# Graph attention and slice attention on one core: tokens interleaved by four, two more transposes by blocks and DMA, a new planner

## The chip, the cores and the metric

The kernel runs on one core of a Trainium2 chip. A core has TensorE (PE, matmuls, with a separate path PEld that loads weights), VectorE (DVE), ScalarE (ACT), GpSimd (POOL) and SyncE (SP, which here only issues DMAs). All run their own instruction queues in order and wait for each other by semaphores. The metric is device time in microseconds (us). The time before is 2927.27 us, the median of 3 runs (2927.26 to 2929.62).

## The reference

`x` has 32 batches of 512 tokens with 256 features, all in float32. Each batch goes through a graph block and a slice-attention block, each with a residual. Cut to what matters:

```python
# graph block, on xn = layernorm(x)
out = relu(xn @ mlp1_w + mlp1_b);  residual = out              # 256 -> 512
h = out @ W_fc                                                 # 512 -> 512
att = softmax(leaky_relu(f1[:, :, None] + f2[:, None, :]))     # f1, f2: h times halves of a_fc
out = elu(elu(att @ h)) + residual
out = relu(out @ mlp2_w + mlp2_b);  residual = out             # 512 -> 256
h = out @ W_hand
e = where(adj > 0, leaky_relu(f1[:, :, None] + f2[:, None, :]), -9e15)
x = x + relu(elu(elu(softmax(e) @ h)) + residual)
# slice block, on xn = layernorm(x), 8 heads, 64 slices each
w = softmax((xn @ W_x + b_x) @ W_slice / temperature)          # 512 tokens x (8 heads x 64 slices)
token = (w.T @ (xn @ W_fx + b_fx)) / (sum of w over tokens)
out_slice = softmax(q @ k.T / 8) @ v                           # q, k, v from token, per head
x = x + (w @ out_slice) @ W_out + b_out
```

Outputs are all of `x`, in float32.

## The kernel before

**Tiling.** A batch's 512 tokens are four tiles of 128 (`NT = 4`), tile `t` holding tokens `t*128` to `t*128+127`. Tensors exist with tokens on the partitions (`xn`, `h`, `e`, `w`, `u`) or with features on them (`xnT`, `o0T`, `o1T`, `o2T`, `xn2T`, `wT`, with 512 token columns). A matmul contracts over partitions, so several tensors must be transposed. Weights are folded at the start: `weff`, `beff` (W_x with W_slice), `wqk`, `wvo` (W_v with W_out), and the columns of `wfc` and `wh` that give f1 and f2.

**Stages of a batch**, in the order in which the code records them:
- `front(b)`: load (`xt`), layernorm to `xn`, transpose to `xnT`; mlp1 to `o0T` (lines 606 to 613); `h` (616 to 627); the factors `fm`, `f2m`, `ex`, `acb`, with transposes on TensorE (628 to 657); `pT`, the unnormalised attention of the first graph layer, from two products on VectorE (659 to 667); attention times h and the double elu to `u` (671 to 682), transposed and added to `o0T` to give `o1T` (683 to 687).
- `middle(b)`: mlp2 to `o2T`; `h` of the second layer (`h2`); `f2b`, a broadcast row made by four TensorE transposes; the residual `r2`, `o2T` transposed back by eight TensorE transposes (717 to 723); per tile of tokens `e` on VectorE, its exp on ScalarE, and four TensorE transposes and a copy into `p2T` (728 to 743); p2T times h, elu, and the sum into `x1`.
- `back(b)`: layernorm, `xn2T` by eight TensorE transposes, the slice weights `w` with their softmax, `wT` by 16 TensorE transposes; the sums `s1` over tokens, `s1T` by eight TensorE transposes; the token block `pm` (lines 832 to 839): for each of four head pairs `p` and two `k` a matmul of 128 x 128, of which only the two 64 x 64 diagonal blocks are used, and one bias matmul from the four rows of `bfx` and `nrow`; then scores `psc`, `attbd`, `vo`, `gg`, and the output.

**Transposes through DRAM.** `xn` and `u` are transposed without TensorE: `flip` (line 355) is one VectorE instruction that transposes each 32 x 32 block inside 128 x 256 or 128 x 512, writing runs of 32 elements; `gather` (361) then writes the four groups of 32 partitions with four DMAs into a scratch tensor in DRAM and reads them back with one, so that the blocks land in their places. The token columns come back in the order (a t i), and `in_order` and `as_gathered` are views that read them in the order needed.

**What sets the order.** No engine order is written out by hand. `Recorder` records every operation, and `_schedule` (115) simulates the engines with the costs of `_cost` (90), list scheduling by a key. The key is the batch number plus a share of the batch's TensorE work; `order` (227) tries 45 combinations of three parameters (`ORDERS`) and takes the one with the shortest `_length`. A DMA is reckoned as 0.1 us on its issuer and a landing after 2.5 us plus its bytes over 180 GB/s, each alone. `AHEAD = 3` lets a batch start while the oldest unfinished is up to three behind. The program is emitted in that order, with semaphores (line 255, so all instructions carry this line in the profile).

**Queues.** All loads of `x`, all scratch DMAs and the output are issued by SP, in the planned order: an issue that waits holds back all that follow. Some weights are loaded from ScalarE's queue at the start. PSUM has five `mm` buffers, two `tr` and one `sm`.

Of the kernel before, what the change touches and what calls it, by code (L numbers as in the profile page):

```python
# [14 lines left out]
ENGINES = ("tensor", "vector", "scalar", "gpsimd", "sync")  # L15
P = 128
# [4 lines left out]
class Recorder:  # L21
# [4 lines left out]
    DRAIN = 0.17  # L26
    KEPT = 1
    AHEAD = 3
    ORDERS = (1.0, 1.1, 1.2, 1.3, 1.4), (1.2, 1.4, 1.6), (0.0, 0.1, 0.2)

    def __init__(self, nc):
        self.nc, self.ops, self.logs, self.age, self.stage = nc, [], {}, -1, 0
        for engine in ENGINES:
            setattr(self, engine, _Recording(self, engine))
# [24 lines left out]
    def take(self, engine, method, args, kwargs):  # L59
# [4 lines left out]
        op = _Op(engine, method, args, kwargs, self.age, self.stage, len(self.ops))  # L64
        op.cost, op.lag = self._cost(op, outs[0], ins)
        before = {}
        for aps, writes in ((ins, False), (outs, True)):
            for ap in aps:
# [4 lines left out]
                op.logs.add(log)  # L73
# [16 lines left out]
    def _cost(self, op, out, ins):  # L90
# [6 lines left out]
        if op.method == "dma_start":  # L97
            return 0.1, 2.5 + out.size() * 4 / 180e3
        if op.engine == "tensor":
            one = max(n / 1200 + 0.002, 0.109)  # L100
            return (one if op.method == "transpose" else 2 * one), self.DRAIN
# [13 lines left out]
    def _schedule(self, ops, key, spare):  # L115
# [34 lines left out]
        done = []  # L150
        while len(done) < len(ops):
# [22 lines left out]
            free[op.engine] = t + op.cost  # L174
            for log in op.logs:
                users[log] -= 1
                until[log] = max(until[log], op.end)
                if not users[log]:
                    slots[log.tag].append(until[log] + self.SIGNAL + spare)
# [17 lines left out]
    def _length(self, ops):  # L197

        free, ready, users, until, slots, held = {}, {}, {}, {}, {}, set()
        for op in ops:  # L200
            for log in op.logs:
                users[log] = users.get(log, 0) + 1
        for op in ops:
            at = ready.get(op, 0.0)
            for log in op.logs:
                if log not in held:
                    held.add(log)
                    places = slots.setdefault(log.tag, [0.0] * log.bufs)
                    places.sort()
                    at = max(at, places.pop(0))  # L210
            t = free.get(op.engine, 0.0)
            t = max(t + (0.03 if op.engine == "tensor" and at > t - 0.1 else 0.0), at)
            free[op.engine], end = t + op.cost, t + op.cost + op.lag
            for log in op.logs:
                users[log] -= 1
                until[log] = max(until.get(log, 0.0), end)
                if not users[log]:
                    slots[log.tag].append(until[log] + self.SIGNAL)
            for later in op.after:
                if later.engine != op.engine:  # L220
                    at = end + self.SIGNAL
                else:
                    at = t + op.cost if op.engine == "tensor" else end
                ready[later] = max(ready.get(later, 0.0), at)
        return max(free.values())

    def order(self):

        work, parts = {}, {}
        for op in self.ops:
            stage = op.age, op.stage
            parts[op] = work.get(stage, 0.0)
            work[stage] = parts[op] + (op.cost if op.engine == "tensor" else 0.0)
        best = None
        for late, long, spare in product(*self.ORDERS):
            turns = {
                op: op.age + (late + long * part / work[op.age, 1] if op.stage else
                              part / (work[op.age, 0] or 1.0))  # L240
                for op, part in parts.items()
            }
            try:
                ops = self._schedule(self.ops, turns.get, spare)
            except RuntimeError:
                continue
            length = self._length(ops)
            if best is None or length < best[0]:
                best = length, ops
        self.length = best[0]  # L250
        return best[1]
# [6 lines left out]
class _Log:  # L258


    def __init__(self, ap, age):
        tensor = ap.tensor
        self.name, self.tag, self.bufs = tensor.name, tensor.tag, tensor.tag_meta.bufs
        self.psum = ap.space == bass.MemoryType.PSUM

        self.queue = self.tag, age if self.psum else 0
        self.entries = []


class _Op:  # L270
    def __init__(self, engine, method, args, kwargs, age, stage, index):
        self.engine, self.method, self.args, self.kwargs = engine, method, args, kwargs
        self.age, self.stage, self.index = age, stage, index
        self.logs, self.after = set(), []
# [17 lines left out]
def adj_ffn_kernel(  # L292
# [59 lines left out]

    Q = 32

    def flip(src, stage, t):

        nc.vector.transpose(
            stage[:, :, ts(t, Q)], src.rearrange("p (c i) -> p c i", i=Q)
        )

    def gather(stage, dst):


        blocks = stage.shape[1]
        scr = dram.tile([blocks, Q, P // Q, P], F32, name="scr", tag=f"scr{blocks}", bufs=2)
# [8 lines left out]
    def in_order(cols):  # L374

        return cols.rearrange("p (a t i) -> p t a i", a=P // Q, t=NT)

    def as_gathered(cols):

        return cols.rearrange("p (t a i) -> p a t i", a=P // Q, t=NT)  # L380
# [4 lines left out]
    def row(name, shape=(P, 512)):  # L385
        return new(name, shape, bufs=2)
# [11 lines left out]
    def load_x(b):  # L398
        if b < B:
            xt[b] = new("xt", [P, NT, D], bufs=2)  # L400
            nc.sync.dma_start(xt[b], x[b].rearrange("(t p) d -> p t d", p=P))
# [14 lines left out]
    for s in range(2):  # L416
        nc.scalar.dma_start(
            wfc[:, :, s, :HH], W_fc[:, ts(s, HH)].rearrange("(k p) f -> p k f", p=P)
        )
    w2 = new("w2", [P, KH, D])  # L420
# [5 lines left out]
    nc.sync.dma_start(wh[:, :, :D], W_hand.rearrange("(k p) f -> p k f", p=P))  # L426
    wfx = new("wfx", [P, KD, INNER])
# [27 lines left out]

    for a, width in ((a_fc, HID), (a_hand, D)):
        ab = med("ab", (P, 2, HID))
        nc.sync.dma_start(
            ab[:, :, :width],
            bass.AP(tensor=a.tensor, offset=a.offset, ap=[[0, P], [width, 2], [1, width]]),  # L460
        )
        for k in range(width // P):
            for s in range(2):
                scr = row("m")
                if width == HID:
                    w_k, wa = wfc[:, k, :, :HH], wfc[:, k, s, HH : HH + 1]
                    a_s = ab[:, s, :].rearrange("p (s f) -> p s f", s=2)
                    scr_k = scr.rearrange("p (s f) -> p s f", s=2)
                else:
                    w_k, wa = wh[:, k, :D], wh[:, k, D + s : D + s + 1]  # L470
                    a_s, scr_k = ab[:, s, :D], scr[:, :D]
                nc.vector.scalar_tensor_tensor(
                    scr_k, w_k, 1.0, a_s, op0=OP.mult, op1=OP.mult, accum_out=wa
                )

    adjt = new("adjt", [P, NT, N], tag="w", dtype=I32)
    nc.sync.dma_start(adjt, adj.rearrange("(t p) j -> p t j", p=P))
    for t in range(NT):
        nc.vector.tensor_scalar(mbias[:, t, :], adjt[:, t, :], 0.0, None, op0=OP.is_gt)
# [95 lines left out]
    def transpose_features(src, dst):  # L575

        for k in range(KD):
# [3 lines left out]
            nc.scalar.copy(dst[:, k, :], pt)  # L581
# [13 lines left out]
    def front(b):  # L595

        load_x(b + 1)
        xn = new("xn", [P, NT, D])
        layernorm(xt[b], xn, "ln1")
        stage = new("xn_stage", [P, D // Q, P])  # L600
        for t in range(NT):
            flip(xn[:, t, :], stage, t)
        xnT = new("xnT", [P, KD, N])
        gather(stage, xnT)
        o0T = new("o0T", [P, KH, N], bufs=2)
        for m in range(KH):
            pm = mm_tile([P, N])
            for k in range(KD):
                nc.tensor.matmul(
                    pm.rearrange("p (t a i) -> p t a i", t=NT, i=Q), w1[:, k, ts(m)],  # L610
                    in_order(xnT[:, k, :]), start=(k == 0), stop=(k == KD - 1),
                )
            nc.scalar.activation(o0T[:, m, :], pm, AF.Relu, bias=b1[:, m : m + 1])


        h = new("h", [P, NT, 2, HH + 1])
        for t in range(NT):
            for s in range(2):
                pm = mm_tile([P, HH + 1])
                for k in range(KH):  # L620
                    nc.tensor.matmul(
                        pm, o0T[:, k, ts(t)], wfc[:, k, s, :], start=(k == 0), stop=(k == KH - 1)
                    )
                if s:
                    nc.vector.tensor_copy(h[:, t, s, :], pm)
                else:
                    nc.scalar.copy(h[:, t, s, :], pm)
        f1, f2 = h[:, :, 0, HH], h[:, :, 1, HH]

# [28 lines left out]

        pT = new("pT", [P, NT, N])
        for j in range(NT):  # L660
            nc.vector.tensor_scalar(
                pT[:, j, :], acb[:, 1, :], ex[:, 3, j : j + 1], None, op0=OP.mult
# [5 lines left out]

        o1T = new("o1T", [P, KH, N])
        stage = new("u_stage", [P, HID // Q, P], tag="p2T")  # L670
        for i in range(NT):
# [11 lines left out]
            flip(u, stage, i)  # L683
        gather(stage, o1T)
        for m in range(KH):
            o1 = o1T[:, m, :].rearrange("p (a t i) -> p a t i", t=NT, i=Q)
            nc.vector.tensor_tensor(o1, o1, as_gathered(o0T[:, m, :]), op=OP.add)
        return o1T

    def middle(b, o1T):  # L690

        o2T = new("o2T", [P, KD, N])
        for m in range(KD):
            pm = mm_tile([P, N])
            for k in range(KH):
                nc.tensor.matmul(
                    pm.rearrange("p (t a i) -> p t a i", t=NT, i=Q), w2[:, k, ts(m)],
# [271 lines left out]
```

## Time and profile before

| what | us |
|---|---|
| median of three runs | 2927.27 |
| the profiled execution's own time | 2928.26 |
| its span, first to last instruction | 2926.5 |
| TensorE busy with matmuls | 2853.9 |
| VectorE busy | 1978.3 |
| ScalarE busy | 1119.3 |
| mean granted TensorE clock | 0.996 of full |

Rows of the page that matter for the change, each with count, busy us and mean ns of one:

| engine, row | count | busy us | mean ns |
|---|---|---|---|
| PE `tr<-ident,e` | 512 | 76.8 | 273 |
| PE `tr<-ident,o2T` | 256 | 43.6 | 273 |
| PE `mm<-s1T,wfx` | 512 | 80.9 | 275 |
| PE `mm<-nrow,bfx` | 64 | 35.9 | 640 |
| DVE `u_stage<-u` (flip, 128x512) | 128 | 88.9 | 695 |
| DVE `xn_stage<-xn` (flip, 128x256) | 128 | 49.0 | 421 |
| DVE `pT<-acb,ex` | 128 | 55.8 | 478 |
| DVE `h<-mm` 128x257 | 128 | 54.4 | 425 |
| DVE `h<-mm` 128x258 | 64 | 27.3 | 426 |
| ACT `p2T<-tr` | 128 | 74.9 | 585 |
| ACT `r<-tr` | 64 | 37.4 | 585 |

A matmul of float32 shows as two instructions on TensorE, a transpose as one. The mean of one includes the time in which it overlaps its neighbours in the pipeline, so the distance between starts is shorter than the mean. "Idle before" is time of that engine alone; only idle time of the engine that bounds the kernel costs time.

### The profile page before, as it was taken

How to read it: one execution, taken by the hardware profiler on the slowest of the kernel's cores; microseconds unless marked ns; L12 is line 12 of the kernel's file. 1: busy time of each engine (PE TensorE's matmuls, PEld its weight loads, DVE VectorE, ACT ScalarE, POOL GpSimd, SP SyncE). 2: the span in 40 equal slices, each digit the busy share in tenths (PEclk: the TensorE clock that was granted, in tenths of full speed). 3: DMA queues.
4: the chain of work that ended last, by engine and by line, in shares of the span. 5: the costliest groups of instructions: out<-in, count | busy, mean ns of one | idle time of the engine just before them, and what ended most of it. 6: DMA issues, size and time to landing. Idle time of an engine off the chain costs nothing.

```text
span 2926.5 us, 35159 instructions
## 1 busy us (share of the span) xinstructions
PE 2853.9 (98%) x13037; PEld 2187.4 (75%) x13037; DVE 1978.3 (68%) x4694; ACT 1119.3 (38%) x2182; POOL 112.8 (4%) x233
## 2 busy tenths in 40 slices
PE   3999999999999999999999999999999999999997
PEld 3777777777778777778777778777777777777775
DVE  4567776667776666776676866677766677766675
ACT  1433444333443343443333443333433334433432
POOL 1000000000000000000000000000000000000000
PEclk9999999999999999999999999999999999999998
DMA  5112220112211122211122211122201122201110
GB/s 177 44 29 65 65 65 22 52 57 65 65 53 34 44 65 65 65 44 44 44 65 65 65 36 51 44 65 65 65 26 54 51 65 65 61 19 45 43 44 15
DMA packets 185412, 159.34 MB, mean 54 GB/s; under 512 B 9109, under 2 KB 159257, under 8 KB 185241
## 3 DMA queue, kind: packets, MB, share of 16 engines
q1 hardware_dynamic: 181904, 154.96, 18.0%
q10 hardware_dynamic: 3336, 2.14, 0.3%
q8 instruction: 103, 1.69, 0.2%
q14 instruction: 69, 0.56, 0.1%
HBM read 89.96 MB, written 67.11 MB: 54 GB/s over the span
## 4 chain that ended last, share of the span: by engine, by line
PE 95%; DVE 3%; DMA 1%; ACT 0%; issue 0%; SPq 0%; POOL 0%; ACTq 0%; POOLq 0%; DVEq 0%
PE mm L255 85%; PE tr L255 9%; PE sm L255 1%; DVE w L255 1%; DVE mx L255 0%; DVE rs L255 0%; DMA wfx<-in_L_ffn_W_fx_dram 0%; DMA temp<-n_L_ffn_temperature_dram 0%; DVE m L255 0%; DVE u L255 0%; DMA scr<-xn_stage 0%; ACT m L255 0%; DMA xt<-in_x_dram 0%; DVE pT L255 0%; DVE ln_st L255 0%
## 5 line engine op out<-in xcount | busy, mean ns | idle before, releaser
L255 PE MATMUL mm<-wfc,o0T 128*128 128x257 f32 x2048 | 579.0, 381 | 0.0
L255 PE MATMUL mm<-h,pT 128*128 128x257 f32 (+1 forms) x2048 | 454.6, 378 | 0.1
L255 PEld LDWEIGHTS mm<-h,pT 128*128 128x128 f32 x2048 | 386.1, 189 | 80.5 <-issue 13.4
L255 PEld LDWEIGHTS mm<-wfc,o0T 128*128 128x128 f32 x2048 | 363.7, 190 | 53.2 <-issue 16.3
L255 PE MATMUL mm<-gg,wT 128*128 128x256 f32 x1024 | 299.5, 379 | 0.0
L255 PE MATMUL mm<-h,p2T 128*128 128x256 f32 x1024 | 290.8, 379 | 0.0
L255 PE MATMUL mm<-xnT,w 128*128 128x512 f32 x512 | 249.3, 592 | 0.0
L255 PE MATMUL mm<-xn,w 128*128 128x257 f32 x1024 | 246.4, 382 | 0.0
L255 PE MATMUL mm<-o1T,w 128*128 128x512 f32 x512 | 241.2, 592 | 0.0
L255 PE MATMUL mm<-weff,xn2T 128*128 128x512 f32 x512 | 226.7, 596 | 0.7 <-ACT xn2T L255 0.7
L255 DVE COPY h<-mm 128x257 f32<-128x257 f32 (+1 forms) x192 | 81.7, 425 | 208.2 <-PE mm L255 204.2
L255 PEld LDWEIGHTS mm<-gg,wT 128*128 128x128 f32 x1024 | 189.2, 190 | 24.0 <-ACT gg L255 0.2
L255 PEld LDWEIGHTS mm<-h,p2T 128*128 128x128 f32 x1024 | 186.6, 190 | 24.5
L255 PEld LDWEIGHTS mm<-xn,w 128*128 128x128 f32 x1024 | 186.0, 192 | 23.7 <-issue 3.3
L255 PEld LDWEIGHTS mm<-weff,xn2T 128*128 128x128 f32 x512 | 97.8, 191 | 122.9 <-issue 99.8
L255 ACT ACTIVATE m<-m 128x512 f32<-128x512 f32 x192 | 120.9, 630 | 170.7 <-DVE m L255 170.6
L255 DVE SCALAR_TENSOR_TENSOR u<-m,u 128x512 f32<-128x512 f32 x192 | 131.5, 685 | 70.3 <-ACT m L255 70.3
L255 ACT ACTIVATE u<-mm,rd 128x256 f32<-128x256 f32 x192 | 90.3, 470 | 208.0 <-PE mm L255 181.2
L255 ACT COPY h<-mm 128x257 f32<-128x257 f32 (+1 forms) x192 | 71.8, 374 | 227.2 <-PE mm L255 224.7
L255 PE MATMUL mm<-wh,o2T 128*128 128x258 f32 x512 | 155.6, 390 | 0.0
L255 ACT ACTIVATE w<-w 128x512 f32<-128x512 f32 x128 | 80.8, 631 | 187.6 <-DVE w L255 187.6
L255 ACT ACTIVATE o2T<-mm,b 128x512 f32<-128x512 f32 x64 | 44.0, 687 | 263.2 <-PE mm L255 262.9
(141 smaller groups left out, 4396.6 us busy)
## 6 DMA issues: line engine op xcount, KB each, us to landing
scr<-u_stage SPq DMA_DIRECT2D x128, 256.0 KB, 4.0
o1T<-scr SPq DMA_DIRECT2D x32, 1024.0 KB, 5.7
xt<-in_x_dram SPq DMA_DIRECT2D x32, 512.0 KB, 4.6
x<-in_x_dram SPq DMA_DIRECT2D x32, 512.0 KB, 4.1
scr<-xn_stage SPq DMA_DIRECT2D x128, 128.0 KB, 2.4
xnT<-scr SPq DMA_DIRECT2D x32, 512.0 KB, 6.4
out_dram<-x SPq DMA_DIRECT2D x32, 512.0 KB, 3.2
w<-in_L_gnn_mlp_w_dram SPq DMA_DIRECT2D x2, 512.0 KB, 6.8
```

What stands on the lines that cost most here:

```text
L255: getattr(getattr(self.nc, op.engine), op.method)(*op.args, **op.kwargs)
```

## The change

1. **Interleaving.** Tile `t` now holds tokens `t`, `t+4`, `t+8`, ... (`"(p t) d -> p t d"` in loads, in the adjacency and in the store). Transposed tensors hold tokens in plain order; a tile's columns are `every(cols, t)`, that is `cols[:, t::4]`, every fourth element, 16 bytes apart. The flips write `stage[:, :, t::4]`, also every fourth element. Matmuls that used to read their moving operand through `in_order` read it plainly; matmuls whose stationary operand is a tile's columns (`o0T`, `o2T`, `p2T`, `xn2T`, `wT`) now read it 16 bytes apart.
2. **`e` and the residual through DRAM.** `e` and `o2T` (for `r2`) join `xn` and `u` in the tuple `FLIPPED` and go by flip and gather; for `o2T` the scratch rows are 64 elements wide. In the first and last batch (`EDGES`) all four are transposed by TensorE.
3. **Token block.** Sixteen matmuls of 64 x 64, one per head and `k`, each into its half of the PSUM partitions, in place of eight of 128 x 128; the bias as two matmuls with 64 output rows; `tok` is one copy.
4. **ScalarE takes over** the first product of `pT` and all copies of `h`.
5. **The planner.** Keys are given per named step in a table `TURNS`, first with a fixed `PERIOD`; a schedule of the first batches gives the starts of batch `SAMPLE`, which are then repeated with the measured period for all batches, shifted at the ends by `HEAD` and `TAIL`. Transfers are reckoned as one queue (`moved`): each begins 1.2 us after its issue or when the one before has moved. `xt` has one buffer in place of two, and the load of a batch is recorded with that batch. Set-up that the first batch doesn't need is a step of its own with a later key.

The diff, cut to its core:

```diff
+TURNS = {
+    "load": -251.8, "norm1": -181.8, "mlp1": -125.6, "h": -118.6, "factors": -118.6,
+    "p": -104.1, "pv": -104.0, "o1": -104.0, "mlp2": -45.4, "h2": -45.4, "e": -44.3,
+    "p2": -44.3, "pv2": -33.3, "norm2": -27.9, "w": 39.5, "sums": 44.1, "s1T": 70.8,
+    "tokens": 71.0, "att": 76.0, "vo": 99.5, "gg": 99.5, "out": 117.0,
+}
+PERIOD, SPARE = 83.2, 0.08
+HEAD, TAIL = (-13.9, -9.7, -5.6), (0.9, 2.5, 8.7)
+SAMPLE, SETUP = 8, 15.0
+FLIPPED = ("xn", "u", "e", "o2")
...
+    ISSUE, BEGIN, LAND, BEHIND = 0.45, 1.2, 0.9, 3.0
...
-            return 0.1, 2.5 + out.size() * 4 / 180e3
+            side = next(ap for ap in (out, *ins) if ap.space != bass.MemoryType.DRAM)
+            op.moving = out.size() * 4 / (250e3 if side.ap[0][1] <= P // 4 else 320e3)
+            return self.ISSUE, 0.0
...
+            if out.ap[0][1] == P // 2:
+                one = max(n / 2400, 0.03)
...
+            if op.moving:
+                moved = max(moved, t + self.BEGIN) + op.moving
+                op.end = moved + self.LAND
+                free[op.engine] = max(t + op.cost, moved - self.BEHIND)
...
-    def flip(src, stage, t):
-        nc.vector.transpose(
-            stage[:, :, ts(t, Q)], src.rearrange("p (c i) -> p c i", i=Q)
-        )
+    def flip(src, dst):
+        nc.vector.transpose(dst, src.rearrange("p (c i) -> p c i", i=Q))
+
+    def by_dma(what, b):
+        return what in FLIPPED and b not in EDGES
...
+    def every(cols, t):
+        return cols[:, t::NT]
...
+    def transpose_features(what, b, src, dst):
+        if by_dma(what, b):
+            stage = new(what + "_stage", [P, D // Q, P], tag="stage4")
+            for t in range(NT):
+                flip(src[:, t, :D], stage[:, :, t::NT])
+            gather(what, stage, dst)
+            return
...
-                        pm, o0T[:, k, ts(t)], wfc[:, k, s, :], start=(k == 0), stop=(k == KH - 1)
+                        pm, every(o0T[:, k], t), wfc[:, k, s, :],
+                        start=(k == 0), stop=(k == KH - 1),
                     )
-                if s:
-                    nc.vector.tensor_copy(h[:, t, s, :], pm)
-                else:
-                    nc.scalar.copy(h[:, t, s, :], pm)
+                nc.scalar.copy(h[:, t, s, :], pm)
...
-            nc.vector.tensor_scalar(
-                pT[:, j, :], acb[:, 1, :], ex[:, 3, j : j + 1], None, op0=OP.mult
+            nc.scalar.activation(
+                pT[:, j, :], acb[:, 1, :], AF.Copy, scale=ex[:, 3, j : j + 1]
             )
...
+            if by_dma("e", b):
+                flip(e, stage[:, :, i::NT])
+                continue
             pt = tr_tile([P, NT, P])
             for j in range(NT):
                 nc.tensor.transpose(pt[:, j, :], e[:, ts(j)], ident)
-            nc.scalar.copy(pT[:, :, ts(i)], pt)
+            nc.scalar.copy(pT[:, :, i::NT], pt)
+        nc.step = "p2"
+        if by_dma("e", b):
+            gather("e", stage, pT)
...
+        if by_dma("o2", b):
+            stage = new("o2_stage", [P, N // Q, KD * Q], tag="stage4")
+            for k in range(KD):
+                nc.vector.transpose(
+                    stage[:, :, ts(k, Q)].rearrange("p (t c) i -> p t c i", t=NT),
+                    o2T[:, k, :].rearrange("p (c i t) -> p t c i", t=NT, i=Q),
+                )
+            gather("o2", stage, r2)
...
-                        pm[:, s, :], pT[:, j, ts(i)], h[:, j, :D],
+                        pm[:, s, :], every(pT[:, j], i), h[:, j, :D],
...
-        pm = mm_tile([P, NP, P])
+        pm = mm_tile([P, NP, G])
         for p in range(NP):
             for k in range(KD):
-                nc.tensor.matmul(
-                    pm[:, p, :], wfx[:, k, ts(p)], s1T[:, k, ts(p)],
-                    start=(p == 0 and k == 0), stop=False,
-                )
-        nc.tensor.matmul(pm, bfx, nrow, start=False, stop=True)
+                for s in range(2):
+                    nc.tensor.matmul(
+                        pm[ts(s, C), p, :], wfx[:, k, ts(2 * p + s, C)],
+                        every(s1T[:, k], p)[:, ts(s, G)],
+                        start=(p == 0 and k == 0), stop=False,
+                    )
+        for s in range(2):
+            nc.tensor.matmul(
+                pm[ts(s, C)], bfx[:, ts(s, C)], nrow[:, s], start=False, stop=True
+            )
...
-                        po[:, s, :], wT[:, p, ts(t)], gg[:, p, :],
+                        po[:, s, :], every(wT[:, p], t), gg[:, p, :],
```

The order of the changed program, without times, can be read from the built program; the prediction counts instructions in it. Per inner batch SP then issues, in this order: four `xn_stage` writes, four `e_stage` writes, the gathers of `xnT` and `p2T`, four `u_stage` writes, the gather of `o1T`, the output, the loads of `xt` and `x1`, four `o2_stage` writes and the gather of `r2`.

## The prediction
> **What bounds the kernel now.** I read the busy shares first, then the chain of waits, then one batch by windows, then the order of time inside it.
>
> ```profile
> PE 2853.9 (98%) x13037; PEld 2187.4 (75%) x13037; DVE 1978.3 (68%) x4694; ACT 1119.3 (38%) x2182; POOL 112.8 (4%) x233
> PE 95%; DVE 3%; DMA 1%; ACT 0%; issue 0%; SPq 0%; POOL 0%; ACTq 0%; POOLq 0%; DVEq 0%
> q1 hardware_dynamic: 181904, 154.96, 18.0%
> ```
>
> TensorE is busy 98% and is 95% of the chain; VectorE has a third of its time free and the transfers are thin. In windows from one batch's `fm` transpose to the next, columns as the page names them:
>
> ```profile
> 1013.53:1102.02 88.49, 88.49 (x408) 67.95 (x406) 61.17 (x146) 34.90 (x68) 3.41 (x7) 1.00 0.19 54
> 2606.29:2694.78 88.49, 88.49 (x408) 67.94 (x407) 61.36 (x146) 34.90 (x68) 3.41 (x7) 1.00 0.16 48
> 0.00:60.00 60.00, 15.65 (x62) 11.00 (x63) 29.47 (x111) 5.21 (x9) 7.85 (x18) 1.00 0.64 194
> ```
>
> A batch takes 88.49 us with no idle TensorE, so 32 x 88.49 = 2832 of the 2926.5 us are dense matmul. The first 60 us hold only 15.65 of TensorE: 44 us are idle there. The rest is the tail, with some 25 us idle. A matmul can be priced from the timeline by the distance of starts:
>
> ```profile
> 1091.62 0.60 PE L255 MATMUL tr<-ident,e 128*128 128x128 f32 x4
> 1092.06 0.60 PE L255 MATMUL mm<-wfc,o0T 128*128 128x257 f32 x2
> 1092.49 0.59 PE L255 MATMUL mm<-gg,wT 128*128 128x256 f32 x2
> ...
> 1072.12 0.60 PE L255 MATMUL mm<-wfc,o0T 128*128 128x257 f32 x2
> 1072.65 1.12 PE L255 MATMUL mm<-nrow,bfx 4*128 4x512 f32 x2
> 1073.70 0.70 PE L255 MATMUL mm<-wh,o2T 128*128 128x258 f32 x2
> ```
>
> Four transposes 0.434, so 0.109 each; a matmul of 256 or 257 columns (two instructions) 0.433; one of 512 about 0.857; of 128 columns 0.22. The bias matmul from four rows takes 1.15 from 1072.55 to 1073.70, although two streams of 512 columns need 0.86: 0.29 is lost around it.
>
> The transfers behind a transpose through scratch, on SP:
>
> ```profile
> 1044.31 3.45 SPq L255 DMA_DIRECT2D scr<-u_stage  x4
> 1051.14 0.38 SPq L255 DMA_DIRECT2D o1T<-scr  x1
> o1T<-scr SPq DMA_DIRECT2D x32, 1024.0 KB, 5.7
> xt<-in_x_dram SPq DMA_DIRECT2D x32, 512.0 KB, 4.6
> ```
>
> The gather waits for the writes' landings: 6.8 from first issue to it, then 5.7, so 12.5 us for 1 MB there and back.
>
> **What the Trainium skill says.** "TensorE: Matmul & The Clock Gate", LDWEIGHTS: a load costs its columns over 1.2 GHz, 107 ns for 128. The trace agrees (0.109 per transpose, where load and stream are equal). "Advanced Engine Details and Errata", Memory Cachelines: SBUF has 16-byte lines and a different line at each access carries a penalty, unpriced. No access in the trace of before shows a large operand stepping 16 bytes. "TensorEngine Tiling (Array Packing)", Key Properties: changing the tiling mode drains TensorE, and tiles run in parallel. The 0.29 around the four-row matmul fits the drain; parallel tiles are not shown.
>
> **The change part by part**, per inner batch unless said.
>
> 1. The 16 transposes of `e` and 8 of `o2T` leave TensorE: 24 x 0.1086 = -2.61. Over 30 batches -78.
> 2. The first and last batch get TensorE transposes of `u` (16) and `xn` (8): +2.6 each, +5.
> 3. Token block. Before: 8 matmuls of 128 columns at 0.22 = 1.76, plus 1.15, together 2.91. After: 16 of 64x64, sequentially 0.11 each by halving load and stream (1.76), overlapped halves 0.88; I take 1.4. The bias comes as two matmuls with other work between them: 2 x (0.43 + 0.29) = 1.44. The 64-column mode is entered and left twice, because a 512-column matmul stands before the sixteenth in the order: 2 x 0.29 = 0.58. Sum 3.42, so +0.5, from -1.2 (0.88 + 0.86, no drains) to +0.9 (3.78). Over 32, +16.
> 4. Strided operands. o0T, p2T, o2T, xn2T and wT are now loaded as every fourth column. A load may take up to one stream, 216 ns for 256 columns against 109 now, before it shows. Below: it cannot gain. Price taken 0; at three times, 327 ns, the 144 loads of a batch that stand before 256 to 258 columns lose 111 ns each = 16 us.
> 5. VectorE. Added: four flips of e and two of o2 at 0.695 = 4.2. Removed: four `tensor_scalar` of pT (0.478), four copies of h (0.425), two of h2 (0.426), to ScalarE = 4.5. So about 61 of 88 stays. ScalarE gains 4 x 0.63 (the row of w's exp), 4 x 0.374 and 2 x 0.374, loses six copies at 0.585: 36 of 88. Neither is a bound while the strided writes of the flips cost nothing; at twice, see the rivals.
> 6. Waits for DMA. The order of instructions puts, from the last transpose of f2b to the first p2 matmul, 51 matmuls of 257 columns, 2 of 256, 4 of 512 and 22 transposes = 22.1 + 0.9 + 3.4 + 2.4 = 28.8 us. In that time: ScalarE's f2b copy and hops 1.4; VectorE's queue up to the last flip of e (four times add, max, reduce, flip at 0.68 + 0.62 + 0.61 + 0.62, means less the 0.07 by which neighbours overlap; four xn flips at 0.35; three w instructions 1.4) 12.9; the wait for the last exp about 1.6; then writes 6.8, gather 5.7, and about 1 because xnT's 512 KB gather stands before p2T's on SP. Sum 29.4 against 28.8: p2 waits 0.6. For `u` to mlp2: 25.1 of TensorE (13 transposes 1.4, token 3.4, ten of 512 8.6, pq 0.4, scores 0.9, eight of 256 3.5, out 6.9) against 6.4 of elu (its second exp queues behind an o0T on ScalarE) + 12.5 + four adds 2.5 = 21.4: hidden. I take 0.7 for both, from 0 to 4. Behind p2 stands all of TensorE's queue, so the wait is paid in full. Over 30, +21. The other new issues on SP (four e writes, four o2 writes, two gathers, 10 x 0.45 us) and 3 MB more per batch (DMA share 0.19 to about 0.3) are hidden: r2 is needed a whole p2 later. If that cover goes, it is the same wait.
> 7. Head. Before, the layernorm of the first tile waits on VectorE behind `temp` (20.3 us idle) and TensorE until 42.9. After, x is first (0.7 + 4.6), statistics 2.3, POOL 1.9, apply 1.4, eight transposes at the cold 0.24 and the first copies: mlp1 at about 14. Up to the first `fm` the order has 10 of 512, 32 of 257 and 5.8 us of setup = 28.3, plus 4 cold and 2 waiting for wx: 48 against 75.5, -27. In the fill of the next two batches I give 4 back, as nothing covers the new DMA round trips there: -23 (from -32 to -10).
> 8. The tail has the same serial chain (layernorm, softmax, tokens): 0, from -8 to +8.
>
> Sum: -78 + 5 + 16 + 21 - 23 = -59. Against the profiled span 2926.5 (2928.26 with what lies around it; the median shown is 2927.27, so it stands for the median): about **2867**; I say 2866.
>
> **Rivals.**
> A, better: halves of the array overlap without drains (-1.7 x 32 = -54) and the DMA arrives in time (-21): 2791. For it: the transfers' margin is within an error of 1 us. Against: the 0.29 seen at the four-row matmul.
> B, slower: the flips write every fourth element, 16 bytes apart, and take twice. Four flips of e (+0.62 each) and four of xn (+0.35 each) stand in VectorE's queue on the way from f2b to p2, which has no slack: +3.9 per batch, 30 x 3.9 = +117: 2983. It decides from 2.0 us per batch, flips at 1.5 times. For it: the skill's lines; against: a flip now runs at 0.695 per 512, one element per cycle, and needs no more than one write per cycle.
> C, the wait takes the saving's place: transfers and hops are 2 us later than summed, because e's writes meet xn's on the queue. p2 then waits 2.7: 2926, no change.
> D, loads of strided weights at three times: 32 x 16 = +510, 3376. From 230 ns per load on it eats the gain. That the matmuls simply don't get fewer is excluded: the order shows it.
>
> **How the numbers follow.** Mine 0.40 (2810 to 2915), A 0.19, B 0.19, C 0.14 (0.05 faster, 0.03 same, 0.06 slower), D 0.08. Faster by over 0.2% (6 us, about what a measurement can tell): 0.40 + 0.19 + 0.05 = 0.64; same 0.03; slower 0.06 + 0.19 + 0.08 = 0.33. The range leaves out D, and the edges of A and B: 2785 to 2990. My own case alone: 2810 to 2915.
>
> **What would show it.** `fm` to `fm` at 87.1 with 0.7 of TensorE idle before p2; first `fm` near 48; no `tr<-ident,e` but in two batches; flips at 0.695; loads of o0T at 190 ns as now; the 64x64 block and its bias at 3.4. Wrong if the flips or the loads lengthen, if TensorE waits over 3 us per batch for p2T or o1T, or if the head keeps its 40 idle us.

## The result and the profile after

| | us | ratio to before (95% interval) |
|---|---|---|
| before, median of 4 runs beside it | 2928.44 (2927.26 to 2930.5) | |
| changed, median of 4 runs | 2974.26 (2973.24 to 2976.06) | 1.0156 (1.0139 to 1.0174) |
| predicted | 2866 | |

The change makes the kernel 1.6% slower. The page of the changed kernel (busy time, share and instructions of each engine; the chain that ended last; the main DMA queue):

```profile
PE 2929.7 (99%) x12941; PEld 2391.9 (80%) x12941; DVE 2088.7 (70%) x4634; ACT 1270.3 (43%) x2298; POOL 127.9 (4%) x233
...
q1 hardware_dynamic: 295056, 243.06, 28.3%
...
PE 80%; DMA 10%; DVE 4%; ACT 2%; SPq 2%; issue 2%; ACTq 0%; POOL 0%; POOLq 0%; DVEq 0%
```

TensorE has 96 matmul records fewer than before and is busy 76 us longer; PEld, the loading of the stationary operand, gained 205 us. The chain now goes through DMA for 10%, but a chain also follows a transfer that arrives just in time. What TensorE really lost by waiting is in its list of waits (us in total, times, longest):

```profile
PE mm L255 <- DMA p2T<-scr: 12.5, 23, 1.1
PE tr L255 <- DVE xn L255: 8.7, 1, 8.7
PE mm L255 <- DVE attT L255: 3.5, 2, 2.4
```

The new wait for p2T is 12.5 us in the whole kernel, far too little. One inner batch by windows (us, then PE, PEld, DVE, ACT and POOL with their counts, TensorE clock, DMA share, GB/s):

```profile
1079.83:1170.66 90.83, 90.72 (x401) 74.05 (x400) 65.39 (x145) 39.09 (x71) 3.97 (x7) 1.00 0.30 87
```

Before, a batch took 88.49 with 408 matmul records; now 401 take 90.83 with TensorE busy throughout. So single matmuls became longer. From the `fm` marks of both traces:

| us | before | after | difference |
|---|---|---|---|
| start to the first `fm` | 75.5 | 49.7 | -25.8 |
| first to fourth `fm` | 230.1 | 219.5 | -10.6 |
| 28 batches, fourth to last `fm` | 2478.7 (88.52 each) | 2547.4 (90.98 each) | +68.7 |
| last `fm` to the end | 142.2 | 156.1 | +13.9 |

The edges gain 22.5 us together. The steady part loses 2.46 us per batch where a gain of about 1.4 had been forecast (2.61 less 0.5 and 0.7). The loads by stationary operand (count, busy us, mean ns), first of the kernel before, then of the changed one:

```profile
L255 PEld LDWEIGHTS mm<-h,pT 128*128 128x128 f32 x2048 | 386.1, 189 | 80.5 <-issue 13.4 <-DVE pT L255 7.2 <-PE mm L255 6.7
L255 PEld LDWEIGHTS mm<-wfc,o0T 128*128 128x128 f32 x2048 | 363.7, 190 | 53.2 <-issue 16.3
L255 PEld LDWEIGHTS mm<-gg,wT 128*128 128x128 f32 x1024 | 189.2, 190 | 24.0 <-ACT gg L255 0.2
```

```profile
L255 PEld LDWEIGHTS mm<-wfc,o0T 128*128 128x128 f32 x2048 | 494.1, 326 | 15.6 <-issue 7.2
L255 PEld LDWEIGHTS mm<-h,pT 128*128 128x128 f32 x2048 | 383.6, 190 | 54.2 <-issue 2.7 <-DVE pT L255 0.7
L255 PEld LDWEIGHTS mm<-gg,wT 128*128 128x128 f32 x1024 | 246.8, 329 | 10.0
```

pT, still loaded from neighbouring columns, stays at 190 ns; o0T and wT, now every fourth column, went to 326 and 329. The price on TensorE is the distance of starts. In the timeline of the changed kernel (start, us, group) the 32 instructions of `gg,wT` stand in one run:

```profile
1128.04 7.65 PE L255 MATMUL mm<-gg,wT 128*128 128x256 f32 x32
1135.52 1.02 PE L255 MATMUL mm<-o1T,w 128*128 128x512 f32 x2
```

(1135.52 - 1128.04) / 32 = 0.234 us each, against 0.217 (0.433 for two) before. The load has outgrown the stream of 256 columns under which it was hidden. Summing starts to starts over one batch each (before, after): `wfc,o0T` 14.03, 15.12; `p2T` 6.93, 7.68; `gg,wT` 6.91, 7.49; `weff,xn2T` 6.87, 7.38; `wh,o2T` 3.65, 3.82. Together +3.1 us a batch, 99 us over 32. In the same way the token block went from 2.91 to 3.85, +0.94. Waits for p2T add 0.4 (the 12.5 us of the list over 30 batches) to 0.55 (what the distance of starts ahead of p2 holds beyond its matmuls). With -2.61 for the removed transposes that gives +1.8 to +2.0 of the 2.46; the rest was not taken apart.

### The profile page after: what moved, and what is told of

It is laid out like the page before. It is cut to its first block, busy times and chain, and to the rows that moved or that the text cites. A ratio compares the mean times of both kernels' runs of the same rounds, so it can differ in the third digit from the quotient of the medians.

```text
span 2972.7 us, 35238 instructions
## 1 busy us (share of the span) xinstructions
PE 2929.7 (99%) x12941; PEld 2391.9 (80%) x12941; DVE 2088.7 (70%) x4634; ACT 1270.3 (43%) x2298; POOL 127.9 (4%) x233
## 4 chain that ended last, share of the span: by engine, by line
PE 80%; DMA 10%; DVE 4%; ACT 2%; SPq 2%; issue 2%; ACTq 0%; POOL 0%; POOLq 0%; DVEq 0%
PE mm L255 74%; DMA p2T<-scr 5%; PE tr L255 5%; DMA scr<-e_stage 4%; SPq L255 2%; DVE e_stage L255 1%; PE sm L255 1%; ACT wT L255 1%; ACT e L255 1%; DVE e L255 1%; DVE u L255 0%; DMA wfc<-in_L_gnn_W_fc_dram 0%; DMA wx<-in_L_ffn_W_x_dram 0%; ACT m L255 0%; DVE nmax L255 0%
## 5 line engine op out<-in xcount | busy, mean ns | idle before, releaser
L255 PE MATMUL mm<-wfc,o0T 128*128 128x257 f32 x2048 | 513.2, 401 | 0.0
L255 PEld LDWEIGHTS mm<-wfc,o0T 128*128 128x128 f32 x2048 | 494.1, 326 | 15.6 <-issue 7.2
L255 PE MATMUL mm<-h,p2T 128*128 128x256 f32 x1024 | 258.1, 404 | 12.7 <-DMA p2T<-scr 12.5
L255 ACT COPY h<-mm 128x257 f32<-128x257 f32 (+1 forms) x384 | 144.6, 376 | 283.4 <-PE mm L255 277.7
L255 PEld LDWEIGHTS mm<-h,p2T 128*128 128x128 f32 x1024 | 244.8, 328 | 24.6 <-DMA p2T<-scr 22.4
L255 PEld LDWEIGHTS mm<-gg,wT 128*128 128x128 f32 x1024 | 246.8, 329 | 10.0
L255 PE MATMUL mm<-gg,wT 128*128 128x256 f32 x1024 | 247.3, 398 | 0.0
L255 DVE TENSOR_SCALAR u<-mm,rd 128x256 f32<-128x256 f32 x192 | 90.7, 472 | 154.1 <-PE mm L255 145.7
L255 PEld LDWEIGHTS mm<-o1T,w 128*128 128x128 f32 x512 | 97.7, 191 | 107.8 <-issue 105.1
L255 ACT COPY wT<-tr 128x512 f32<-128x512 f32 x128 | 140.4, 1097 | 62.6 <-PE tr L255 62.4
L255 PEld LDWEIGHTS mm<-weff,xn2T 128*128 128x128 f32 x512 | 144.2, 317 | 25.1 <-ACT xn2T L255 3.7
```

Source lines behind the costliest of these rows:

```text
L255: getattr(getattr(self.nc, op.engine), op.method)(*op.args, **op.kwargs)
```

## The experiments

The kernel before, run beside each, had medians of 2927.67 (the first four), 2928.46 (the next four) and 2928.02 us (the last four), so the times can be compared with each other and with 2974 for the changed kernel. Theory 1: the 16-byte step in what TensorE reads is the price. Theory 2: the moved transposes, with their slow strided writes and the waits they bring, are. In e1, e2, e3 and e12 the columns of different tokens get mixed up: the work and its shapes are those of the changed kernel, the values are not. "Steady us per batch" is the stretch from the fourth to the last `fm`, over 28.

| run | us | ratio (95% interval) | steady us per batch |
|---|---|---|---|
| e1_loads_plain | 2911.98 | 0.9947 (0.9933 to 0.9962) | 89.16 |
| e2_writes_plain | 2952.09 | 1.0083 (1.0068 to 1.0098) | 90.26 |
| e3_loads_step2 | 2912.71 | 0.9949 (0.9934 to 0.9964) | 89.10 |
| e4_tokens_128 | 3421.25 | 1.1683 (1.1658 to 1.1707) | 104.87 |
| e5_tokens_128_same_order | 3017.50 | 1.0304 (1.0289 to 1.0319) | 92.05 |
| e6_only_e_strided | 2877.17 | 0.9824 (0.9810 to 0.9839) | 88.10 |
| e7_only_e_strided_old_tokens | 2886.92 | 0.9855 (0.9839 to 0.9872) | 88.27 |
| e8_planner_alone | 2890.88 | 0.9871 (0.9856 to 0.9886) | 88.48 |
| e9_tokens_read_plain | 2942.39 | 1.0048 (1.0031 to 1.0065) | 90.06 |
| e10_residual_only | 2865.91 | 0.9788 (0.9773 to 0.9802) | 87.60 |
| e11_residual_and_new_tokens | 2834.98 | 0.9681 (0.9666 to 0.9695) | 86.74 |
| e12_loads_and_writes_plain | 2856.05 | 0.9757 (0.9742 to 0.9772) | 87.43 |

**Loads from neighbouring columns.** All weight loads of o0T, o2T, p2T, xn2T and wT:

```diff
+    def own(cols, t):
+        return cols[:, ts(t)]
...
-                        pm, every(o0T[:, k], t), wfc[:, k, s, :],
+                        pm, own(o0T[:, k], t), wfc[:, k, s, :],
```

> Changes only which columns the strided stationary operands take: 128 neighbours in place of every fourth (tokens are then mixed up, so the output is another one; the amount of work is the same). Theory 1 (a load of every fourth column takes 233 ns and so outlasts the 216 ns stream it hides behind): 144 loads x 0.0165 plus the exposed ones, 3.1 us per batch or 99 us in all, go; up to 1.05 us per batch may come back as wait for p2T, since 32 of the loads stand between f2b and p2 and VectorE's chain to p2 stays as it is. So 2875 to 2907, and loads of o0T at 190 ns. Theory 2 (the flips and copies that write every fourth element are slow and make TensorE wait): TensorE then only waits longer, less than 20 us go, 2955 or more.

62 us of the 99 came back, 5 us short of theory 1's range. The loads are at 190 ns again, but new waits stand in TensorE's list, 28 us more on these two lines than in the changed kernel, in whose list the transfer of xnT has no line:

```profile
PE mm L255 <- DMA xnT<-scr: 20.4, 23, 2.6
PE mm L255 <- DMA p2T<-scr: 19.9, 22, 1.6
```

With TensorE faster, transfers that had been in time come late: part of the load's price is paid back as waiting. Whether the slow writes on the way to those transfers are the reason is asked of e12.

**Writes in runs.** The flips of xn, u and e and the copies of ScalarE write neighbouring columns, and the flip of o2T, which had stepped where it reads, reads neighbouring ones:

```diff
-                flip(e, stage[:, :, i::NT])
+                flip(e, stage[:, :, ts(i, Q)])
...
-            nc.scalar.copy(wT[:, :, t::NT], pt)
+            nc.scalar.copy(wT[:, :, ts(t)], pt)
```

> Changes only where the flips on VectorE and the copies on ScalarE write: runs in place of every fourth element (tokens are then mixed up, same amount of work). Theory 1: only the waits that TensorE has for p2T can go, 0.4 to 0.75 us per batch, so 2945 to 2970, although VectorE gets some 5 us and ScalarE some 4 us per batch lighter. Theory 2: most of the loss goes, below 2895.

2952, 22 us less than the changed kernel: theory 2 is not the main part. The writes had indeed become slow. VectorE's and ScalarE's groups in the changed kernel:

```profile
L255 DVE STREAM_TRANSPOSE e_stage<-e 128x512 f32<-128x512 f32 x120 | 133.4, 1112 | 26.2 <-ACT e L255 26.1
L255 DVE STREAM_TRANSPOSE u_stage<-u 128x512 f32<-128x512 f32 x120 | 132.2, 1102 | 1.0
L255 ACT COPY wT<-tr 128x512 f32<-128x512 f32 x128 | 140.4, 1097 | 62.6 <-PE tr L255 62.4
```

and here:

```profile
L255 DVE STREAM_TRANSPOSE u_stage<-u 128x512 f32<-128x512 f32 x120 | 84.7, 705 | 1.0
L255 DVE STREAM_TRANSPOSE e_stage<-e 128x512 f32<-128x512 f32 x120 | 83.9, 699 | 52.4 <-ACT e L255 52.4
...
L255 ACT COPY wT<-tr 128x512 f32<-128x512 f32 x128 | 74.9, 585 | 84.2 <-PE tr L255 84.0
```

A flip costs 1.6 times as much with the step, a copy 1.9 times, but VectorE at 65 and ScalarE at 39 of 91 us a batch have room for it. What shows is the wait for p2T, which is gone from TensorE's list here.

**A step of 8 bytes.** Loads of every second column:

```diff
+    def own(cols, t):
+        return cols[:, ts(t // 2, 2 * P)][:, t % 2 :: 2]
```

> As e1, but the stationary operands take every second column, 8 bytes apart, so that two of each 16 bytes are used. If the price belongs to a new 16-byte line at every element, as the skill's lines say, loads are at 190 ns again and the time is that of e1 within 5 us. If any step costs, or the price grows with the step, loads lie between 190 and 326 ns and the time between e1 and the changed kernel.

The same time as with neighbouring columns, within 1 us, the waits of that run included. The loads of this kernel:

```profile
L255 PEld LDWEIGHTS mm<-wfc,o0T 128*128 128x128 f32 x2048 | 395.0, 196 | 57.6 <-issue 14.4 <-ACT o0T L255 0.6
...
L255 PEld LDWEIGHTS mm<-gg,wT 128*128 128x128 f32 x1024 | 200.3, 196 | 37.7 <-issue 11.9 <-ACT gg L255 7.1
```

196 ns at 8 bytes, 326 at 16: it isn't the stride as such. The price sets in somewhere above 8 bytes and at 16 at the latest; a step of 12 was not run.

**The token block put back**, 128 x 128 as before, and the planner left to order the result:

> Undoes only the token block: eight matmuls of 128x128 and one bias matmul. By the slots of the trace of after the block costs 3.85 us per batch against 2.91 in the trace of before, so 0.94 x 32 = 30 us go: 2944. By the prediction's step 3 it would be 16 us: 2958. If halves ran side by side with profit, it gets slower, 2980 or more.

3421. The expectation held the edit for a local one, but the planner, given another list of operations with the same table `TURNS`, made another order for all of TensorE. No single wait stands out (the three longest in total are 53.9, 45.4 and 39.5 us, none above 1.1 us at a time). So the run says nothing about the block. The same block was then exchanged at the moment of writing out, so that the order is the changed kernel's:

```diff
+                whole = ("tensor", "matmul", (
+                    pm[:, p, :], wfx[:, k, ts(p)], every(s1T[:, k], p),
+                ), dict(start=first, stop=False))
...
+                        start=first, stop=False, instead=[] if s else [whole],
```

> The changed kernel with the token block alone put back to eight matmuls of 128x128, one bias matmul and two copies, but in the changed kernel's own order of instructions: planned as the new block, exchanged as it is written out. If the token block costs what its rows show (3.85 us a batch against 2.91, 0.94 each, with the two changes of TensorE's tile shape in it): 2974 - 30 = 2944 us, period 90.0. If the block lies beside a wait for the flips anyway, the wait takes the saving: 2965 to 2975, period 90.7 to 91.0. If it is worth only what I had forecast, 0.5 a batch: 2958.

All three numbers were wrong, in sign too: 43 us slower than the changed kernel, so the old form would have been worse there. (Against the run before, with the same operations in another order, it is 404 us faster: that is the order alone.) The block's row before, in the changed kernel, and here:

```profile
L255 PE MATMUL mm<-s1T,wfx 128*128 128x128 f32 x512 | 80.9, 275 | 0.3 <-ACT s1T L255 0.3
```

```profile
L255 PE MATMUL mm<-s1T,wfx 128*64 128x64 f32 x1024 | 78.9, 297 | 2.5 <-ACT s1T L255 2.4
```

```profile
L257 PE MATMUL mm<-s1T,wfx 128*128 128x128 f32 x512 | 125.0, 408 | 2.1 <-ACT s1T L257 1.8
```

The same instruction takes 275 ns with s1T in neighbouring columns and 408 with every fourth. Here s1T is the moving operand, which streams through the array, and nothing hides it. That led to a third theory (1a): a strided moving operand costs too. The new block pays less for the same step because its halves run side by side, as the run with the residual and the new block shows below: the starts of single instructions in the trace are 117 ns apart for a pair of 64-wide halves in the changed kernel, and 230 ns apart for one of 128 here.

**Steps only where e needs them.** Everything except p2T's loads and e's flips is put back into neighbouring columns, s1T included; x and out keep their interleaved rows:

```diff
-                        pm, every(o0T[:, k], t), wfc[:, k, s, :],
+                        pm, o0T[:, k, ts(t)], wfc[:, k, s, :],
...
-                flip(u, stage[:, :, i::NT])
+                flip(u, stage[:, :, ts(i, Q)])
...
-                        every(s1T[:, k], p)[:, ts(s, G)],
+                        s1T[:, k, ts(2 * p + s, G)],
```

> The changed kernel, in its order of instructions, with tokens interleaved by four for e alone: x, out, the scores, the flips of xn and u and the weight loads of o0T, o2T, xn2T, wT and s1T run over neighbouring columns as in the kernel before; what stays strided are the 32 loads of p2T and the four flips of e per batch. Theory 1 (the strided loads are the price): of the 3.1 us a batch 0.75 stays with p2T, 2.35 goes: 2974 - 75 = 2899 us, period 88.6, loads of o0T, o2T, xn2T and wT back at 190 ns; 2885 to 2912. Theory 2 (the moved transposes and their waits are the price, not the stride): e and the residual still go by DMA, so the period stays over 90: 2945 to 2975.

2877: 97 us less than the changed kernel, with e and the residual still going by DMA and p2T still loaded by steps. Theory 2 falls as the main cause. The run undoes loads, s1T's read and most strided writes together; e9 and e12 part them. It is 22 us better than expected, mainly because s1T's read, 32 us by its row (78.9 to 47.0), had not been in the sum; waits for p2T and xnT grew by 15 (20.5 and 6.8 against 12.5 and none). The same with the old token block, s1T in neighbouring columns:

> The run above with the token block put back as well, in the same order of instructions. Prices that add: 2899 - 30 = 2869 us, period 87.7, faster than the kernel before by 2%. If the wait for p2T takes what is freed: as the run above less 10 or nothing, 2885 to 2899.

2886.92, 10 us slower, not 30 faster: the 0.94 a batch was not the form of the block. Nor does this run show the new form to be the better one: in the steady part it is 0.17 us a batch ahead (88.10 against 88.27), and 8 of the 10 us stand behind the last `fm` (147.1 against 155.2).

**The planner alone**: blocks of tokens, old token block, e and residual on TensorE, but the new ordering and the TensorE transposes in the first and last batch; the copies and products that ScalarE took over stay there too:

```diff
-FLIPPED = ("xn", "u", "e", "o2")
+FLIPPED = ("xn", "u")
```

> The changed kernel's planning alone (transfers reckoned as one queue, first and last batch by TensorE): tokens in blocks, old token block, e and the residual transposed by TensorE as before. Head 25 us shorter as in the changed kernel, period as before (88.5), tail as before: 2929 - 25 = 2904 us. If the new order of instructions itself lengthened the period, by up to the 2.5 us that the changed kernel lost: 2904 + 28 x 2.5 = 2974.

2890.88, and the period of before to 0.04 us: 13 us better than expected. The planner, with ScalarE's share, costs nothing in the steady part and brings the edges (first `fm` at 48.7 instead of 75.5, first to fourth 215.6 instead of 230.1).

**s1T alone** in neighbouring columns, all else as changed (its copy on ScalarE, and the view in the token block shown above):

> The changed kernel with s1T alone written and read in neighbouring columns (its moving operand in the sixteen small matmuls of the token block), all else and TensorE's order as in the changed kernel. Theory 1a: a strided moving operand costs too; the row of those matmuls fell from 78.9 us (297 ns each) to 47.0 (227) where s1T was plain: 32 us, so 2974 - 32 = 2942, period 90.0. Rival: the 0.94 a batch is the switch of tile shape, and the row's fall comes from the other parts of that run: 2965 to 2975.

2942.39, the expected number, with TensorE's order unchanged. Theory 1a is shown: 32 us for a step of 16 bytes in sixteen small matmuls per batch. A pair of their halves now starts every 58 ns, not every 117. The row (columns as above):

```profile
L255 PE MATMUL mm<-s1T,wfx 128*64 128x64 f32 x1024 | 47.7, 229 | 0.8 <-ACT s1T L255 0.8
```

**The residual alone by blocks and DMA**, on top of the planner:

```diff
-FLIPPED = ("xn", "u")
+FLIPPED = ("xn", "u", "o2")
```

> Planner alone (2891) with one part of the change added: the residual by 32x32 blocks and DMA, its eight transposes per batch gone, tokens in blocks, e on TensorE, token block old. Nothing is strided, and the transfer has half a batch of slack: 8 x 0.109 x 32 = 28 us, 2863; period 87.6. Rival: what the DMA path frees comes back as a wait, as with p2T: 2875 to 2891.

2865.91; the period falls by 0.88, the price of eight transposes at 0.109 (0.87), and nothing comes back as a wait. With the new token block as well, s1T plain:

> The run above with the token block in its new form (sixteen matmuls of 64x64) and s1T in neighbouring columns. In the same order of instructions the new form was 10 us faster: 2853, period 87.3. If the planner, which takes the new block for 1.2 us cheaper than the old, packs a batch tighter than the engines keep, a wait appears: 2863 to 2880.

2834.98, the best kernel here, 3.2% faster than before. The block brings 31 us and not 10. The planner made a new order for it, and the block's own time on TensorE shows why. First the run before, then this one:

```profile
1074.36 1.05 PE L255 MATMUL mm<-s1T,wfx 128*128 128x128 f32 x8
...
1077.40 0.44 PE L255 MATMUL tr<-ident,xn 128*128 128x128 f32 x2
```

```profile
1064.62 0.80 PE L255 MATMUL mm<-s1T,wfx 128*64 128x64 f32 x20
1065.35 0.33 PE L255 MATMUL tr<-ident,xn 128*128 128x128 f32 x1
...
1066.11 0.65 PE L255 MATMUL mm<-nrow,bfx 4*64 4x256 f32 x4
1066.69 0.33 PE L255 MATMUL tr<-ident,xn 128*128 128x128 f32 x1
```

The block with its bias, and one transpose in the midst of each, took 3.04 us (1074.36 to 1077.40) and takes 2.07 (1064.62 to 1066.69); 0.09 more go to the change of tile shape ahead of it. That is 0.88 a batch, 28 of the 31 us. The reason is that the two halves of the array run side by side: twenty instructions of 64 columns start within 0.73 us, where one after the other, at half of the 0.109 for 128 columns, they would need 1.09; the four of the bias take 0.58 for four streams of 256 columns, which one after the other take 0.87. By the single starts the two halves begin 6 to 7 ns apart. In the changed kernel other work stood between the two bias matmuls:

```profile
1113.48 0.64 PE L255 MATMUL mm<-nrow,bfx 4*64 4x256 f32 x2
1114.05 0.44 PE L255 MATMUL tr<-ident,xn 128*128 128x128 f32 x2
```

There each half takes 0.57 alone, 1.14 for both, and the tile shape changes twice as often. Halves gain only where the order leaves them next to each other. One batch of the best kernel by windows:

```profile
947.20:1034.00 86.80, 86.80 (x417) 66.06 (x416) 59.84 (x141) 38.20 (x75) 3.45 (x7) 1.00 0.24 67
```

More matmul records than the changed kernel (417 against 401 a batch), no idle TensorE, and 4 us less: fewer instructions isn't less time.

Next to e6 this run also says what moving `e` was worth. Its 16 transposes, 1.74 us a batch or 52 over 30, are gone in e6; but there p2T's strided loads cost 0.74 a batch (22 us), and the waits for p2T and xnT are 27 us, none of which stands in this run's list. That is a sum from two traces in different orders, and no run moves `e` alone, but by it the way through DRAM gained next to nothing for `e`, where it gained all of its transposes for the residual.

**Loads and writes together** from neighbouring columns (both edits above; s1T is still read with the step):

> The changed kernel with both the weight loads and the writes of flips and copies in neighbouring columns (s1T is still read with a step of four; tokens are mixed up, so the values are not the reference's). The loads alone gave 62 us of the 99 that their slots add, with 28 us more of waits on p2T and xnT. If the slow flips and copies are what made those waits, both together give the 99 and the 12 of waits that the changed kernel has: 2855 to 2875. If the loads are worth only 62: 2974 - 62 - 22 = 2890.

2856.05, within the range of the first expectation. The two edits alone gave 62 and 22 us, together 118. Starting from plain writes, the loads are worth 2952 - 2856 = 96, as their distances of starts had said (99); starting from plain loads, the writes are worth 2912 - 2856 = 56. The planner's order of the first and last batches moved in this run; by the steady part alone, where the order is the same, the loads are worth 90.26 - 87.43 = 2.83 a batch (91 us over 32) and the writes 89.16 - 87.43 = 1.73 (55). The waits of e1 are nearly gone:

```profile
PE mm L255 <- DMA p2T<-scr: 5.4, 13, 1.0
```

## Why the prediction was wrong

By its own steps:

1. Right. The transposes are gone; a transpose was worth 0.109 us, as the run with the residual alone shows.
2. and 8., with 7.: the edges gained 22.5 us where -23 + 5 + 0 was written. The first `fm` came at 49.7 (48). The fill gained 10.6 instead of losing 4, and the stretch after the last `fm`, forecast at 0, lost 13.9. The sum hid two errors; the planner's shift of the last batches moves that mark, and I did not take the tail apart.
3. The term was mis-sized, and for a reason it doesn't name. It put +0.5 a batch; measured is +0.94. It took 1.4 us for the sixteen small matmuls, by halves of load and stream, and said nothing of `every(s1T...)`. They take 1.87, sixteen pairs of halves at 117 ns, and 0.93, at 58 ns, where s1T is plain: the step costs 0.94 a batch by these starts and 32 / 32 = 1.0 by the run. Without it the sum's lower end for the sixteen (0.88, halves overlapped) was nearly right, and so was rival A's overlap; A's missing drains were not, as the matmul ahead of a change of tile shape still takes some 0.09 us longer.
4. **The step that failed.** "A load may take up to one stream, 216 ns for 256 columns against 109 now, before it shows. Below: it cannot gain. Price taken 0". The threshold was right, and so was rival D's "From 230 ns per load on it eats the gain". The load went past it: the starts are 234 ns apart. 144 loads a batch before 256 to 258 columns lose 17 ns each, and with somewhat more at a few of them 2.6 us in all; 16 loads of xn2T lose another 0.5. That is 3.1 us a batch by the distances of starts; e12 against e2 gives 96 us, 2.83 a batch in the steady part. The upper end, three times the price, was too far, and so D was given 0.08; a value between the ends was not costed. The Trainium skill's page "Advanced Engine Details and Errata", section "Memory Cachelines", was cited for a penalty without a price, and the penalty was then given to the flips alone. The skill's page "SBUF — State Buffer", in the note on cachelines in its section "Door 1: The DMA port swizzle", gives 4 float32 as how far one can stride for free. Read as a step of four, these runs contradict it: a step of two is nearly free (196 ns against 190), a step of four isn't (326). The condition that the same note names, at least two hits per 16-byte line, fits both.
5. Half right. The flips take 1102 to 1112 ns, not 695, yet VectorE (65 of 91 us) and ScalarE (39) are no bounds.
6. Right in size: 0.7 was taken, 0.4 to 0.55 measured. Rival B's flips came (1.6 times, over its 1.5) without its 3.9 us a batch: undoing all strided writes gave 22 us, 0.7 a batch. B's path was compared with a TensorE that isn't slowed itself. Where TensorE is not, the same writes cost 56.

The direction turned on step 4: its 96 us alone exceed the 59 that were forecast as gain. With these 96 and 32 for s1T's read, the forecast of 2866 becomes 2994; the measured 2974 lies 20 us below it. Of these, 15 are step 3 without the step of s1T (0.93 instead of 1.4 for the sixteen matmuls, over 32 batches) and 4.5 the edges (-22.5 instead of -18). That rival B's 2983 lies 9 us from the measured time is luck: its flips lengthened, but the time went to the loads that it left alone. Rival C's mechanism is out as well: waits for transfers are not where the time went.

## What to carry to other kernels

When a change of layout alters the step of an operand, price every instruction that reads or writes it, the loads of TensorE and its moving operands first: here float32 elements 16 bytes apart cost about 1 ns per column more, and a load that had been hidden under its matmul was then the bound. If a transpose is to be saved by an interleaved layout, interleave only the tensor that needs it; here that turned 1.6% slower into 1.8% faster, of which the planner alone gives 1.3%. Then ask whether that tensor pays at all: the best kernel here leaves `e` on TensorE. Put matmuls for the two halves of the array next to each other in the order. To test one part of a kernel whose order a planner makes, keep the order and exchange the instructions, otherwise the planner's answer is measured.

## What was not expected of the hardware

- The step of 16 bytes costs much the same everywhere. Weight load of 128 columns: starts 234 ns apart, against 109 for a load and stream that are equal, about 1.0 ns a column. Moving operand, by starts: 230 - 112 = 118 ns for 128 columns, 0.9 each; 117 - 58 = 59 for a pair of halves of 64, 0.9 each. Copy by ScalarE: 1097 - 585 = 512 for 512 elements, 1.0 each. Block transpose by VectorE: 1102 - 695 = 407 for 512, 0.8 each; the flip of o2T, which steps where it reads, 1108 against 711 with neighbours.
- At 8 bytes the load shows next to none of it: 196 ns against 190. Writes and moving operands at 8 bytes were not tried.
- Slow parts hide each other: slow flips cost 22 us beside slow loads and 56 beside fast ones.
- Two halves of the array do run side by side: a pair of 64-wide matmuls starts 6 to 7 ns apart and the next pair 58 ns after it, where a single half takes 59 ns. A change of tile shape costs some 0.09 us in the instruction ahead of it and 0.05 to 0.1 in the one behind. In an order that splits the two bias matmuls the block costs about what it did before (2.85 us with s1T plain, against 2.91); in one that leaves them side by side it is 0.88 us a batch cheaper.
